# A selective-scan kernel: the order of the quarter loads of delta * u

## The chip, the cores and the metric

The kernel runs on one core of a Trainium2 chip. The time is device microseconds of one execution. Time before: 12,278.37 us, the median of three runs (12,270.65 to 12,295.46). One further execution was taken with the hardware profiler; all views below are of that one.

## The reference

Four layers work on images x of shape (4, 64, 64, 96). The first two (L0, L1) are state-space layers: normalise, project 96 channels to 2 x 192, convolve 3 x 3, and scan the 4096 pixels of each image in K = 4 directions (rows, columns, and both backwards), with 16 states per channel. Cut to the scan, which is where the change lies:

```python
def step(h, inp):
    u, d, b, c = inp
    dA = jnp.exp(d[..., None] * A)
    h = dA * h + d[..., None] * b[:, :, None, :] * u[..., None]
    y = jnp.einsum('bken,bkn->bke', h, c)
    return (h, y)
```

Here u is the convolved image in the order of the direction, d is delta (softplus of a small projection, one value per channel and pixel), b and c are 16 values per pixel, and A is a constant per channel and state. The product d * u doesn't depend on the state: it has one value per image, direction, channel and pixel, and every one of the 16 states needs the same value. Afterwards the four directions are added, normalised, gated and projected back. Layers L2 and L3 are attention without softmax and a quantised two-layer network on the same pixels; the change doesn't touch them.

## The kernel before

The two state-space layers are each done for two pairs of images, which gives four phases one after the other. A phase has three parts: `prepare` (normalisation, convolution, delta, b, c), `scan_phase`, and `finish`, which runs beside the next phase's `prepare`. The token layers L2 and L3 come at the end.

`prepare` leaves its results in DRAM. For every chunk of TC = 512 pixels there is one tensor `delta` (bf16, in three parts that add up to fp32) and one tensor `du` with delta * u in fp32. `du` holds two copies of the same data, copy 0 and copy 1; the first index of the tensor is the copy (lines 160 to 162, written at lines 321 and 322). Within a copy, the second index g runs over the G = 8 combinations of direction and image, then come the channels and the pixels.

`scan_phase` (line 471) cuts the work into units: 8 chunks x 16 blocks of EB = 12 channels, 128 units in a phase, 512 in all. The 128 partitions of a unit are 16 states x 8 combinations g. They fall into four quarters of 32 partitions; a quarter is 4 states x 8 combinations. So each of the 8 rows of `du` is wanted in 4 partitions of each quarter. `load` (line 386) takes the tile h of a unit, 128 x 12 x 512 fp32, issues the load of the delta tile (72 partitions, line 379), and then fills h with six loads on SP's DMA queue (line 401). `load_quarters` reads `du` with a broadcast over 4 states. The middle two quarters (partitions 32 to 95) are filled together, from copy 0 and copy 1; a single quarter is filled from one copy only, copy `first % 2`. Each is split in two halves of 6 channels by the loop over e. One middle load moves 768 KB, one quarter load 384 KB, in rows of 12,288 B.

The loop over a unit's 12 channels n then interleaves these steps on five engines, in an order that is written out by hand (`manual_schedule`):

- POOL multiplies three channels of h by b at a time (`times_b`, line 411), half a unit ahead of the scan. Its first two products of a unit read the first half of h, its last two the second.
- TensorE spreads delta over the states (`replicate`, line 417), ScalarE turns it into exp(delta * A) (`decay`, line 421).
- VectorE runs the recurrence over 512 pixels in place in h (`scan`, line 428), with the carry of the chunk before.
- TensorE contracts the finished unit with c (`contract`, line 446), ScalarE evicts (line 458), and at the end of the unit SP stores y in four pieces (`store`, line 466).

At the last channel of unit `at`, SP issues the store of unit at - 1 and then the loads of unit at + 3 (lines 532 to 539); h has four buffers. So SP's DMA queue holds in each unit one delta load, six h loads and four y stores, and now and then a load of b or c. A DMA takes one of eight semaphores in turn; SP waits before it issues a DMA until the DMA before it on the same semaphore has landed.

Of the kernel before, what the change touches and what calls it, by code (L numbers as in the profile page):

```python
# [82 lines left out]
class Consts:  # L83
# [3 lines left out]
    def load(self, pool, name, shape):  # L87
        t = pool.tile(shape, F32, name=name)
        self.nc.sync.dma_start(t, self.a[name])
        return t  # L90
# [40 lines left out]
class Scans:  # L131
# [19 lines left out]
    def prepare(self, ph):  # L151
# [16 lines left out]
        with self.tc.tile_pool(name="prep", bufs=1) as wp, self.tc.tile_pool(  # L168
# [3 lines left out]
            def load(name, shape, at=0):  # L172
                t = wp.tile([at + shape[0]] + shape[1:], F32, name=name)
                nc.sync.dma_start(t[at:], a[pre + name])
                return t

            xp = load("x_proj", [C, 2, 2, XD2])
            dt_w = load("dt_w", [XD2 - 2 * NS, 2, E], at=2 * NS)
            conv_b = load("conv_b", [C, 2])
            ds = load("Ds", [C, 2, K])  # L180
            dsum = wp.tile([C, 2], F32, name="dsum")
# [204 lines left out]
    def load(self, u):  # L386

        nc, ph = self.nc, u.ph
        u.h = self.units.tile([128, EB, TC], F32, name="h", bufs=4)
        self.load_delta(u)  # L390
        n = EB // 2
        for first, quarters in ((1, 2), (3, 1), (0, 1)):
            for e in range(0, EB, n):
                self.load_quarters(u, e, n, first, quarters)

# [595 lines left out]
```

## Time and profile before

| | |
|---|---|
| median of three runs | 12,278.37 us |
| profiled execution | 12,285.39 us, its span 12,283.6 us |
| scan phases, from first to last scan of each | 784 to 2659, 3596 to 5467, 6406 to 8279, 9215 to 11,088 us |
| VectorE busy in the steady stretch of the first phase (812 to 2540 us) | 1661.90 of 1728 us |
| POOL busy there | 1614.88 us |
| ScalarE busy there | 1182.33 us |
| TensorE matmul busy there, granted clock | 1332.07 us, 0.90 |
| share of the 16 DMA engines there, bytes | 0.74, 252 GB/s |

How to read the views. The profile names engines PE (matmul), PEld (weight load), DVE (VectorE), ACT (ScalarE), POOL (GpSimd) and SPq (SP's instruction queue). A row of the costliest groups gives line, engine, operation, output <- inputs with partitions x elements, the count, busy time in us, mean ns of one, and then the idle time just ahead of it with what ended it. The chain of waits goes back from the last instruction to whatever released it, step by step, and gives shares of the span; "DMA h<-du" there is time between the issue and the landing of an h load. A line of the waits reads: who waited, for whom, us in total, times, longest. A line of the timeline gives start, duration, engine, line, operation and count, and in brackets the idle time before it. A wait for several things is put down to the one that seems to have come last, so a name in brackets may be a neighbour of the true cause. The trace also holds one record for each DMA packet (start, duration, bytes) and one for each part of a load that lands.

### The profile page before, as it was taken

How to read it: one execution, taken by the hardware profiler on the slowest of the kernel's cores; microseconds unless marked ns; L12 is line 12 of the kernel's file. 1: busy time of each engine (PE TensorE's matmuls, PEld its weight loads, DVE VectorE, ACT ScalarE, POOL GpSimd, SP SyncE). 2: the span in 40 equal slices, each digit the busy share in tenths (PEclk: the TensorE clock that was granted, in tenths of full speed). 3: DMA queues.
4: the chain of work that ended last, by engine and by line, in shares of the span. 5: the costliest groups of instructions: out<-in, count | busy, mean ns of one | idle time of the engine just before them, and what ended most of it. 6: DMA issues, size and time to landing. Idle time of an engine off the chain costs nothing.

```text
span 12283.6 us, 340681 instructions
## 1 busy us (share of the span) xinstructions
PE 9393.5 (76%) x147008; PEld 4897.8 (40%) x147008; DVE 9369.7 (76%) x9235; ACT 7066.9 (58%) x11815; POOL 7389.7 (60%) x2316
## 2 busy tenths in 40 slices
PE   7757777769877777769877777778877777777777
PEld 2224444433334444433334444443334444444333
DVE  2479999963569999982569999993459999993667
ACT  2456666643456666653456666662446666662556
POOL 0159999950149999970129999980119999990000
PEclk8669898889778988889778988888778888988787
DMA  3577777754667777764667777764567777773110
GB/s 94 170 226 256 251 252 252 251 166 140 205 206 253 251 252 255 252 201 123 183 206 253 252 251 254 251 226 125 173 194 250 253 253 252 252 252 124 19 21 11
DMA packets 906195, 2491.48 MB, mean 203 GB/s; under 512 B 278030, under 2 KB 560756, under 8 KB 773236
## 3 DMA queue, kind: packets, MB, share of 16 engines
q1 hardware_dynamic: 578036, 2163.43, 52.6%
q10 hardware_dynamic: 326656, 306.25, 8.5%
q8 instruction: 1158, 18.97, 0.7%
q14 instruction: 345, 2.83, 0.1%
HBM read 1955.47 MB, written 513.80 MB: 201 GB/s over the span
## 4 chain that ended last, share of the span: by engine, by line
DMA 57%; PE 20%; SPq 9%; DVE 5%; ACT 4%; issue 3%; POOL 1%; ACTq 1%; DVEq 0%; POOLq 0%
DMA h<-du 51%; SPq L401 8%; PE c L263 8%; PE f L596 2%; PE d L309 2%; DMA yk<-y 2%; DMA delta<-parts 1%; PE c L292 1%; PE f L687 1%; PE f L605 1%; DMA du<-du_sb 1%; POOL parts L323 1%; PE f L676 1%; DVE parts L324 1%; PE f L662 1%
## 5 line engine op out<-in xcount | busy, mean ns | idle before, releaser
L411 POOL TENSOR_TENSOR h<-h,b 128x1536 f32<-128x1536 f32 x2048 | 7019.3, 3461 | 603.8 <-DMA h<-du 230.7
L428 DVE TENSOR_TENSOR_SCAN h<-a,carry,h 128x512 f32<-128x512 f32 x5376 | 6346.6, 1259 | 238.3 <-POOL h L411 231.9
L421 ACT ACTIVATE a<-a,a_col 128x512 f32<-128x512 f32 x6144 | 4030.4, 664 | 1917.7 <-PE a L417 1885.8
L446 PEld LDWEIGHTS y<-h,cw 128*32 128x32 f32 x131072 | 2789.8, 129 | 3520.4 <-issue 1302.1
L446 PE MATMUL y<-h,cw 128*32 128x48 f32 x131072 | 3663.3, 266 | 537.8 <-DVE h L428 210.6
L417 PE MATMUL a<-dlt,rep 72*128 72x512 bf16 x6144 | 2562.4, 428 | 1339.9 <-DVE h L428 1242.8
L323 POOL CAST parts<-dl 96x1024 bf16<-96x1024 f32 x256 | 342.1, 1351 | 3108.6 <-DVE dl L320 2742.6
L319 DVE TENSOR_TENSOR du_sb<-dl,xc 96x1024 f32<-96x1024 f32 x256 | 397.0, 1577 | 1294.6 <-ACT dl L317 1242.0
L458 ACT COPY d<-y 128x384 f32<-128x384 f32 x2048 | 979.7, 478 | 490.5 <-PE y L446 449.4
L263 PE MATMUL c<-xn,taps 96*96 96x512 f32 x2304 | 1036.8, 611 | 73.7 <-DVE xn L248 52.8
L428 DVE TENSOR_TENSOR_SCAN h<-a,h 128x512 f32<-128x512 f32 x768 | 873.0, 1203 | 176.9 <-ACT a L421 139.2
L417 PEld LDWEIGHTS <-rep 72*128 72x128 bf16 x6144 | 490.8, 99 | 888.7 <-issue 646.5
L309 PE MATMUL d<-xd,dt_w 7*96 7x512 f32 x1024 | 523.0, 859 | 260.0 <-ACT xd L295 227.4
L263 PEld LDWEIGHTS c<-xn,taps 96*96 96x96 f32 x2304 | 383.6, 168 | 709.9 <-issue 631.2
L828 POOL MEMSET tn<- 1x4096 f32 x8 | 28.0, 3533 | 863.2 <-PE pa L848 514.2
L270 ACT ACTIVATE xc<-c,conv_b 96x512 f32<-96x512 f32 x128 | 87.3, 682 | 716.0 <-PE c L263 646.4
L596 PE MATMUL f<-yk,perm 128*128 128x384 f32 x1024 | 417.3, 547 | 96.6 <-DMA yk<-y 87.2
L324 DVE TENSOR_TENSOR parts<-dl,parts 96x1024 bf16<-96x1024 f32 x256 | 366.9, 1455 | 154.3 <-POOL parts L323 154.3
L317 ACT ACTIVATE dl<-d 96x1024 f32<-96x1024 f32 x256 | 252.0, 1017 | 402.3 <-DMA delta<-parts 230.6
L292 PE MATMUL c<-xc,x_proj 96*103 96x512 f32 x512 | 422.1, 961 | 2.5 <-ACT xc L270 2.5
L309 PEld LDWEIGHTS d<-xd,dt_w 7*96 7x96 f32 x1024 | 152.3, 212 | 548.3 <-ACT xd L295 299.0
L363 ACT ACTIVATE cw<-c,gmask 128x256 f32<-128x256 f32 x512 | 285.7, 569 | 119.2 <-DMA c<-bc 61.9
(114 smaller groups left out, 5656.7 us busy)
## 6 DMA issues: line engine op xcount, KB each, us to landing
h<-du SPq DMA_DIRECT2D x1024, 768.0 KB
h<-du SPq DMA_DIRECT2D x2048, 384.0 KB
delta<-parts ACTq DMA_DIRECT2D x512, 288.0 KB
dlt<-delta SPq DMA_DIRECT2D x512, 288.0 KB
du<-du_sb SPq DMA_DIRECT2D x256, 384.0 KB
du<-du_sb ACTq DMA_DIRECT2D x256, 384.0 KB
y<-d SPq DMA_DIRECT2D x2048, 48.0 KB
yk<-y SPq DMA_DIRECT2D x256, 384.0 KB
```

The costliest lines, as they stand in the source:

```text
L263: nc.tensor.matmul(rows(ps[:C]), taps[:, tap, h * C : (h + 1) * C], xn[:, ROWS * c + dy : ROWS * (c + 1) + dy, dx : dx + HW], start=tap == ...
L292: nc.tensor.matmul(rows(ps[:XD2]), xp[:, k, h], u[:, h], start=h == 0, stop=h == 1)
L309: nc.tensor.matmul(ps[:, m], dt_w[part, k, m * C : (m + 1) * C], xd[part], start=True, stop=True)
L324: nc.vector.tensor_tensor(parts[:, 2], delta, parts[:, 1], ALU.subtract)
L401: self.nc.sync.dma_start(u.h[32 * first : 32 * (first + quarters), e : e + n].rearrange("p e t -> p (e t)"), source.rearrange("a g e t -> ...
L411: self.nc.gpsimd.tensor_tensor(h, h, b, ALU.mult)
L417: self.nc.tensor.matmul(u.a[n], self.cst.rep[:, h], u.dl[:, e], start=True, stop=True)
L421: self.nc.scalar.activation(u.a[n], u.a[n], AF.Exp, scale=u.ph.a_col[:, at : at + 1])
L428: self.nc.vector.tensor_tensor_scan(u.h[:, n], u.a.pop(n), u.h[:, n], 0.0 if u.c == 0 else u.ph.carry[:, at : at + 1], ALU.mult, ALU.add,)
L446: self.nc.tensor.matmul(view(u.y[32 * j : 32 * j + 32], l2 * EB, (8 * EB, 4), (1, EB)), u.ph.cw[u.c][:, l1, 8 * j + l2], view(u.h, 64 * l1 ...
L458: self.nc.scalar.copy(u.d[:, :, :, l1], u.y[:, : 32 * EB].rearrange("p (t h x) -> p t h x", t=4, h=2))
L596: nc.tensor.matmul(ps[:, : 4 * C].rearrange("p (w v e) -> p w v e", w=4, v=nv), cst.perm[:, k], view(t, off, (sw if k < 2 else -sw, 4), (1 ...
```

## The change

The loop in `load` that fills h names the quarters in another order. Before, after the middle two quarters came quarter 3 (partitions 96 to 127, from copy 1) and then quarter 0 (partitions 0 to 31, from copy 0); now quarter 0 comes ahead of quarter 3. Number, size and issue order of the loads by halves stay as they are.

```diff
@@ -389,7 +389,7 @@
         u.h = self.units.tile([128, EB, TC], F32, name="h", bufs=4)
         self.load_delta(u)
         n = EB // 2
-        for first, quarters in ((1, 2), (3, 1), (0, 1)):
+        for first, quarters in ((1, 2), (0, 1), (3, 1)):
             for e in range(0, EB, n):
                 self.load_quarters(u, e, n, first, quarters)
```

## The prediction

> **What bounds the kernel now.** I read the times first (median 12,278.37 us, three runs from 12,270.65 to 12,295.46; that spread of 0.2% is about what a measurement of this kernel can tell from no change), then the chain of waits and the costliest groups of the page:
>
> ```profile
> DMA 57%; PE 20%; SPq 9%; DVE 5%; ACT 4%; issue 3%; POOL 1%; ACTq 1%; DVEq 0%; POOLq 0%
> DMA h<-du 51%; SPq L401 8%; PE c L263 8%; PE f L596 2%; PE d L309 2%; DMA yk<-y 2%; DMA delta<-parts 1%; PE c L292 1%; PE f L687 1%; PE f L605 1%; DMA du<-du_sb 1%; POOL parts L323 1%; PE f L676 1%; DVE parts L324 1%; PE f L662 1%
> ...
> L411 POOL TENSOR_TENSOR h<-h,b 128x1536 f32<-128x1536 f32 x2048 | 7019.3, 3461 | 603.8 <-DMA h<-du 230.7
> L428 DVE TENSOR_TENSOR_SCAN h<-a,carry,h 128x512 f32<-128x512 f32 x5376 | 6346.6, 1259 | 238.3 <-POOL h L411 231.9
> ```
>
> Half of the chain is the very load that the change reorders; VectorE sat idle mostly for POOL, POOL mostly for that load. Next the queue's own waits of SP, and the timelines of POOL, VectorE and SP in one steady stretch:
>
> ```profile
> SPq L401 <- DMA h<-du: 2362.9, 1448, 3.9
> ```
>
> ```profile
> 1307.83 14.21 DVE L428 TENSOR_TENSOR_SCAN h<-a,carry,h 128x512 f32<-128x512 f32 x12 [0.39 <-POOL h L411]
> 1323.91 38.94 DVE L428 TENSOR_TENSOR_SCAN h<-a,carry,h 128x512 f32<-128x512 f32 x33 [1.87 <-POOL h L411]
> ```
>
> ```profile
> 1320.42 13.68 POOL L411 TENSOR_TENSOR h<-h,b 128x1536 f32<-128x1536 f32 x4 [2.35 <-ACT d L458]
> 1334.28 13.71 POOL L411 TENSOR_TENSOR h<-h,b 128x1536 f32<-128x1536 f32 x4 [0.18 <-DMA h<-du]
> ```
>
> ```profile
> 1331.25 8.01 SPq L401 DMA_DIRECT2D h<-du  x6
> 1339.36 3.24 SPq L466 DMA_DIRECT2D y<-d  x4
> 1343.94 0.81 SPq L379 DMA_DIRECT2D dlt<-delta  x1
> 1345.80 7.89 SPq L401 DMA_DIRECT2D h<-du  x6
> ```
>
> A unit (12 channels x 512 steps) costs VectorE 14.2 us when nothing stops it and POOL 13.7 us. The records of the trace, over 464 steady units (8 to 123 of each phase), give a period of 14.69 us, so about 0.49 us is lost. I call a unit's six h loads m0, m1 (middle 64 rows, first and second half), a0, a1 (next quarter) and b0, b1 (last quarter). In 84% of these units POOL's first product starts within 0.35 us of the landing of b0. The "ACT d" named above is not its cause: the 2.35 us ended when b0 landed. SP holds at most eight loads in flight: m0 of the next unit goes out when a1 has landed, m1 when b0 has landed. So the loads set the pace.
>
> They do so through single DMA engines. m0 and m1 land in 16 parts, each single quarter in only 8 (and one write made at once). The packets of 12,288 B take 460 ns at best (26.7 GB/s), also when 16 engines run; the four quarter loads land 1.87 to 1.90 us apart on the typical engine up to b0, which is 4 x 0.46: the same eight engines do them one after the other. The last engine to land is the one that counts. Its spacings are m0 to m1 1.97 us, to a0 1.88, to a1 1.90, to b0 2.63, to b1 2.47: slow only in the b pair, when the next unit's delta load and m0 have started on the other engines.
>
> [...] At that moment only about three engines carry 12,288 B packets, and these take 0.56 to 0.90 us, so total bandwidth is not the reason.
>
> **The change part by part.** Removed and added: nothing. Every engine issues the same instructions in the same order with the same waits; only the rows and the copy of du behind loads 3 to 6 are exchanged. 2048 loads are touched (512 units x 4), 384 KB each, same issue time. POOL's r0 needs m0, the a and the b of the first half whichever quarter comes last. So at equal transfer speed the step costs 0 us, hidden by nothing because nothing is moved.
>
> [...]
>
> 1. Delta against b, taken away. The b pair of the last engine has 2.63 + 2.47 - 2 x 4 x 0.46 = 1.42 us above the packet times. Part is instruction fetching: 2.11 packets of 16,384 B a unit, at 26.7 GB/s 0.61 us each, spread evenly 2.11 x 0.61 x 5.1 / 14.69 = 0.45 us in that stretch (estimate). 0.97 us is left. [...] -0.97 us a unit. Bounds 0 (the slowness lies on the memory side) to -0.97.
>
> 2. Middle loads against b, added. m0 of the next unit goes out 0.29 us after a1 landed and lands on the typical engine 5.6 us after its issue; the last engine's b0 lands 2.3 us and its b1 4.8 us after that same issue. So b1 lies wholly beside m0. [...] Bounds 0 [...] to +1.84. [...] +1.45 us.
>
> 3. Start of a0 beside the tail of m1's upper half[...]. The last engine reaches a0 late and shows 1.88 us, 0.04 above the packets: at most -0.04 us, taken as 0.
>
> Net 1.45 - 0.97 = +0.48 us a unit on the engine that is never idle: its own packets, 24 x 0.46 + delta 6 x 0.16 + output stores 16 x 0.036 + fetching 1.29, are 13.9 of the 14.69 us. What is late next: b1, hence a0 of the next unit, which SP sends when b1 has landed, then b0, then POOL's first product, then VectorE. Steady units 496 (124 x 4): 496 x 0.48 = 238 us. At each phase start two further units are loaded back to back without a delta gain of note: 4 x 2 x 1.45 = 12 us. Sum 250 us on the profiled execution's own 12,285.39 us (span 12,283.6), 12,535; that run lies 7 us above the median, so 12,528 us.
>
> **The rivals.** (a) [...] both orders meet the same congestion in memory: the same bytes at the same instants, 12,278 us. [...] Against: the b pair is slowed at low total traffic. Chance 0.14. (b) Faster: the delta conflict goes but m0's upper half yields[...]. It decides where the added overlap is below 0.97 us. The gain ends at VectorE's 14.2 us: 496 x -0.49 = -243, 12,035 us; halfway 12,157. Chance 0.22. (c) Much slower: the b pair's 0.97 us was memory, stays, and the whole 1.84 us comes on top: 496 x 1.84 = +913, 13,190 us. Chance 0.07. The forecast itself has 0.57, with its own range from +0.1 us (12,328) to +0.87 us (1.84 - 0.97; 12,278 + 432 = 12,710).
>
> **How the numbers follow.** Slower by over 0.2% holds the forecast and (c): 0.64. Within 0.2% (25 us) holds (a): 0.14. Faster holds (b): 0.22. The range of 8 in 10 runs from 12,130, which leaves out about half of (b), to 12,760, which leaves out (c).
>
> **What would show it.** In the profile after: the same counts in every row of the groups; POOL's mean near 3461 ns and the scan's near 1259 ns; more idle time ahead of L411 and L428; the time that SP waits for h loads at L401 up from 2362.9 us. In the landing records: a0 to a1 still about 1.9 us, a1 to b0 nearer 1.9 than 2.63 (step 1), b0 to b1 well above 2.47 (step 2), period near 15.2 us. Unchanged spacings would mean (a); a b pair under 5.1 us together with a period near 14.2 us would mean (b). [...]

## The result, and the profile after

The changed kernel takes 12,199.1 us (median of four runs, 12,184.87 to 12,209.92) against 12,276.8 us for the kernel before (12,270.65 to 12,295.46): ratio 0.9933, interval 0.9916 to 0.9951. It is faster by 0.67%; forecast was slower by 2.0%. The profiled execution took 12,191.39 us, 94 us less than that of before. From the first to the last scan of each phase, summed over the four phases, the trace gives 7490.6 us before and 7416.3 us after: 74 us of the 94 lie there. The other 20 us lie outside, where nothing was changed; another kernel with the same order (the second experiment) has 4799.6 us outside the scans, against 4793.0 before and 4773.3 after, so this part is what two executions differ by.

The chain of waits and the costliest groups of the changed kernel, the lines that answer to those of before:

```profile
DMA 57%; PE 20%; SPq 9%; DVE 5%; ACT 4%; issue 3%; POOL 1%; ACTq 1%; DVEq 0%; POOLq 0%
DMA h<-du 52%; SPq L401 9%; PE c L263 8%; PE f L596 2%; PE d L309 2%; DMA yk<-y 1%; PE c L292 1%; DMA delta<-parts 1%; PE f L605 1%; PE f L687 1%; PE f L676 1%; POOL parts L323 1%; DVE parts L324 1%; PE f L662 1%; PE ph L806 1%
...
L411 POOL TENSOR_TENSOR h<-h,b 128x1536 f32<-128x1536 f32 x2048 | 7021.7, 3462 | 527.6 <-DMA h<-du 187.1
L428 DVE TENSOR_TENSOR_SCAN h<-a,carry,h 128x512 f32<-128x512 f32 x5376 | 6347.5, 1259 | 176.7 <-POOL h L411 174.0
```

Counts and durations are those of before (3461 and 1259 ns a piece there); only the idle time ahead of the two groups fell, POOL's from 603.8 to 527.6 us and VectorE's from 238.3 to 176.7 us. The loads of h still set the pace: half of the chain is theirs. The page alone can't tell more. SP's own waits, from the queue's view, even point the other way:

```profile
SPq L401 <- DMA h<-du: 2480.7, 1444, 4.4
```

SP waits longer at the h loads than before (2362.9 us), in a faster kernel. So here the wait of the issuing queue does not tell which kernel is slower. The timelines of VectorE and then POOL, in the stretch that was shown of before, are only a sample:

```profile
1299.71 44.73 DVE L428 TENSOR_TENSOR_SCAN h<-a,carry,h 128x512 f32<-128x512 f32 x38
1344.68 36.53 DVE L428 TENSOR_TENSOR_SCAN h<-a,carry,h 128x512 f32<-128x512 f32 x31 [0.23 <-POOL h L411]
```

```profile
1298.13 41.17 POOL L411 TENSOR_TENSOR h<-h,b 128x1536 f32<-128x1536 f32 x12
1341.21 24.13 POOL L411 TENSOR_TENSOR h<-h,b 128x1536 f32<-128x1536 f32 x7 [1.90 <-DMA y<-d]
```

VectorE runs 38 scans without a gap of note, POOL twelve products; then POOL stops for 1.90 us. What ended that stop was b0 of a unit, which landed 0.31 us before the product started; the "y<-d" in brackets is a neighbour.

What tells the kernels apart is the landing records of the h loads. The table has, for 464 steady units, the mean time between the landings of the last DMA engine (m0, m1: middle rows; a0, a1: the single quarter that comes first; b0, b1: the one that comes last; 0 and 1 are the halves), how far the last engine is behind the typical one at b1, and VectorE's period from unit to unit, all in us. The cycle's other three stretches, m0 to m1, m1 to a0 and a0 to a1, are given in the text where they matter. Ratios are to the kernel before. The experiments are in it too.

| kernel | a1 to b0 | b0 to b1 | b1 to next m0 | behind at b1 | period | ratio |
|---|---|---|---|---|---|---|
| before | 2.63 | 2.47 | 3.84 | 3.29 | 14.70 | 1 |
| changed | 2.28 | 3.07 | 3.48 | 3.67 | 14.56 | 0.9933 |
| e1 order of before, copies exchanged | 2.60 | 2.49 | 3.83 | 3.33 | 14.70 | 1.0002 |
| e2 changed order, copies exchanged | 2.32 | 3.08 | 3.46 | 3.72 | 14.57 | 0.9927 |
| e3 order of before, small delta | 1.85 | 1.93 | 4.20 | 1.06 | 14.05 | 0.9732 |
| e4 changed order, small delta | 1.89 | 1.97 | 4.67 | 0.98 | 14.05 | 0.9731 |
| e5 order of before, no upper middle | 2.59 | 2.39 | 3.71 | 3.50 | 14.44 | 0.9896 |
| e6 changed order, no upper middle | 1.98 | 1.97 | 4.30 | 1.39 | 14.06 | 0.9737 |
| e7 order of before, delta between | 3.32* | 1.92 | 2.57* | 1.98 | 14.18 | 0.9784 |
| e8 changed order, delta between | 2.98* | 3.44 | 2.09* | 5.23 | 15.62 | 1.0335 |
| e9 order of before, delta on rows 56 to 127 | 1.93 | 2.42 | 3.89 | 2.32 | 14.14 | 0.9786 |
| e10 changed order, delta on rows 56 to 127 | 2.67 | 3.71 | 3.51 | 4.85 | 15.62 | 1.0359 |

(* The delta load, 6 x 0.16 us on each of its engines, lies in a1 to b0 here, in b1 to m0 elsewhere.)

So the change did shorten a1 to b0 by 0.35 us and lengthen b0 to b1 by 0.60 us, as the prediction said it would; but b1 to the next m0 fell by 0.36 us, m0 to m1 by 0.07, and the period by 0.13 us. Over 512 units that is 67 us of the 74 us that the scan phases got shorter.

### The profile page after: what moved, and what is told of

It reads as the page before. It is cut to its first block, busy times and chain, and to the rows that moved or that the text cites. A ratio compares the mean times of both kernels' runs of the same rounds, so it can differ in the third digit from the quotient of the medians.

```text
span 12189.6 us, 340681 instructions
## 1 busy us (share of the span) xinstructions
PE 9338.7 (77%) x147008; PEld 4884.4 (40%) x147008; DVE 9363.7 (77%) x9235; ACT 7063.0 (58%) x11815; POOL 7391.0 (61%) x2316
## 4 chain that ended last, share of the span: by engine, by line
DMA 57%; PE 20%; SPq 9%; DVE 5%; ACT 4%; issue 3%; POOL 1%; ACTq 1%; DVEq 0%; POOLq 0%
DMA h<-du 52%; SPq L401 9%; PE c L263 8%; PE f L596 2%; PE d L309 2%; DMA yk<-y 1%; PE c L292 1%; DMA delta<-parts 1%; PE f L605 1%; PE f L687 1%; PE f L676 1%; POOL parts L323 1%; DVE parts L324 1%; PE f L662 1%; PE ph L806 1%
## 5 line engine op out<-in xcount | busy, mean ns | idle before, releaser
L411 POOL TENSOR_TENSOR h<-h,b 128x1536 f32<-128x1536 f32 x2048 | 7021.7, 3462 | 527.6 <-DMA h<-du 187.1
L428 DVE TENSOR_TENSOR_SCAN h<-a,carry,h 128x512 f32<-128x512 f32 x5376 | 6347.5, 1259 | 176.7 <-POOL h L411 174.0
L417 PE MATMUL a<-dlt,rep 72*128 72x512 bf16 x6144 | 2529.7, 422 | 1315.1 <-DVE h L428 1228.6
```

The lines of the kernel that those rows point to most:

```text
L411: self.nc.gpsimd.tensor_tensor(h, h, b, ALU.mult)
L417: self.nc.tensor.matmul(u.a[n], self.cst.rep[:, h], u.dl[:, e], start=True, stop=True)
L428: self.nc.vector.tensor_tensor_scan(u.h[:, n], u.a.pop(n), u.h[:, n], 0.0 if u.c == 0 else u.ph.carry[:, at : at + 1], ALU.mult, ALU.add,)
```

## Experiments: is it the rows or the copy?

The change exchanges two things at once: the rows of SBUF that are written and the copy of `du` that is read. The first pair keeps the orders and exchanges the copies alone.

```diff
-        copies = slice(0, 2) if quarters == 2 else slice(first % 2, first % 2 + 1)
+        copies = slice(0, 2) if quarters == 2 else slice(1 - first % 2, 2 - first % 2)
```

> The order of before (quarter 3, then quarter 0), but quarter 3 is read from copy 0 of du and quarter 0 from copy 1. Theory P (what counts is the rows written[...]): nothing changes against before, ratio 1.000 within 0.002, spacings of the last engine a1 to b0 about 2.6 us and b0 to b1 about 2.5 us, period 14.69 us. Theory M (what counts is which copy in DRAM is read late, beside the next unit's middle load): it behaves as the changed kernel, ratio about 0.993, a1 to b0 about 2.3 us, b0 to b1 about 3.1 us.

> The changed order (quarter 0, then quarter 3), with the copies exchanged as in the run before it. Theory P: as the changed kernel, ratio 0.993, a1 to b0 2.3 us, b0 to b1 3.1 us, period 14.56 us. Theory M: as the kernel before, ratio 1.000, a1 to b0 2.6 us. If both matter, each of these two runs lies between.

Measured: e1 is 1.0002 (0.9994 to 1.0010), e2 is 0.9927 (0.9911 to 0.9944). Their spacings agree with those of before and of the changed kernel within 0.04 us. The groups of e1, then of e2:

```profile
L411 POOL TENSOR_TENSOR h<-h,b 128x1536 f32<-128x1536 f32 x2048 | 7020.8, 3462 | 601.5 <-DMA h<-du 227.7
L428 DVE TENSOR_TENSOR_SCAN h<-a,carry,h 128x512 f32<-128x512 f32 x5376 | 6348.1, 1259 | 237.8 <-POOL h L411 234.9
```

```profile
L411 POOL TENSOR_TENSOR h<-h,b 128x1536 f32<-128x1536 f32 x2048 | 7022.0, 3462 | 530.0 <-DMA h<-du 204.9
L428 DVE TENSOR_TENSOR_SCAN h<-a,carry,h 128x512 f32<-128x512 f32 x5376 | 6350.9, 1260 | 174.8 <-POOL h L411 171.7
```

The idle time follows the rows (601.5 and 530.0 us; before 603.8, after 527.6), not the copy. Which copy in DRAM is read makes no difference that these runs can tell.

## Experiments: take each supposed partner of the conflict away

The second pair takes away most of the delta load:

```diff
...
+        if u.c == 0 and u.eb == 0:
+            self.dl0 = self.units.tile([DROWS, DC, TC], BF16, name="dlt", bufs=1)
+            nc.sync.dma_start(self.dl0.rearrange("p e t -> p (e t)"), of)
+        else:
+            few = self.units.tile([DROWS, 128], BF16, name="few", bufs=3)
+            nc.sync.dma_start(few, of[:, :, :128])
+        u.dl = self.dl0
```

> The order of before, but the delta tile is loaded in full only for the first unit of a phase and used for all; every other unit's delta load brings 256 B a row in place of 4096 B (wrong decay in all units but the first, same instructions elsewhere, same number of loads). Theory P: the b pair of the last engine loses its conflict with the delta rows: a1 to b0 falls from 2.63 to about 2.0 us and b0 to b1 from 2.47 to about 2.1 us, the engine also has 0.9 us less of its own, so the period goes to VectorE's own 14.2 us: 512 x 0.45 = 230 us less, about 12,045 us. Theory M: delta takes no part in it; the engine only saves its own 0.9 us, the spacings of the b pair stay near 2.6 and 2.5 us.

> The changed order with the same small delta loads (wrong decay in all units but the first of a phase). Theory P: the changed order had its gain from escaping delta, so nothing of the gain is left: a1 to b0 about 2.0 us as in the run before it, b0 to b1 stays near 3.0 us for the conflict with the upper half of the next middle load, so the b pair is about 0.9 us longer than in the run before it and the time the same or up to 200 us more. Theory M: the b pair keeps the difference that the two full kernels have (0.25 us longer in the changed order), and this run is as fast as the run before it or faster.

Measured: 0.9732 (0.9720 to 0.9745) and 0.9731 (0.9719 to 0.9744), the same. The scan's group in e3, then in e4:

```profile
L431 DVE TENSOR_TENSOR_SCAN h<-a,carry,h 128x512 f32<-128x512 f32 x5376 | 6317.3, 1256 | 0.0
```

```profile
L431 DVE TENSOR_TENSOR_SCAN h<-a,carry,h 128x512 f32<-128x512 f32 x5376 | 6317.3, 1260 | 0.0
```

VectorE has no idle time left ahead of these scans; the period of 14.05 us is its own, 0.15 us less than the 14.2 us that I had read from the timeline. In e3 the b pair fell to nearly the bare packet times (1.85 and 1.93 us against 1.84). That alone does not show delta as the cause: with VectorE setting the pace the loads have slack, and the next unit's m0 is issued 2.39 us after a1 has landed instead of 0.29, so that load is taken away from b as well. The runs that move delta, below, test it by itself. In e4 the expectation that b0 to b1 would stay near 3.0 us is refuted: it is 1.97 us. The last engine is only 1.0 us behind the others instead of 3.7, m0 is issued 2.94 us after a1 instead of 0.35, and its first part lands 3.46 us after b1. So b is over before the next unit's middle load is under way, and the conflict of step 2 does not take place.

The third pair leaves out the upper half of the middle load from the fifth unit of a phase on (the four buffers of h are fixed tiles, whose rows 64 to 95 keep what was there):

```diff
+            if quarters == 2 and i >= 4:
+                quarters = 1
```

> The order of before; from the fifth unit of each phase on, the middle load fills rows 32 to 63 alone[...] (rows 64 to 95 keep what an earlier unit left, so a quarter of the states is wrong; the tile h is four fixed buffers for that). [...] Theory P: [...] nothing changes for the late engine: a1 to b0 about 2.6 us, b0 to b1 about 2.4 us, period 14.6 to 14.7 us, ratio 0.995 to 1.00. A theory in which the late engine suffers from the sheer number of packets in memory: a b pair near 4.2 us and a ratio under 0.98.

> The changed order with the same cut of the middle load. Theory P with the conflict of step 2 [...]: that conflict is gone, b0 to b1 falls from 3.07 to about 2.1 us, the late engine is no longer the limit and the period goes to the 14.03 us seen with small delta loads: ratio about 0.975. If step 2 of the prediction doesn't exist, b0 to b1 stays at 3.0 us and the ratio at 0.993.

Measured: e5 is 0.9896 (0.9880 to 0.9913), e6 is 0.9737 (0.9723 to 0.9752). The scan's group of e5, then that of e6 with its chain of waits:

```profile
L433 DVE TENSOR_TENSOR_SCAN h<-a,carry,h 128x512 f32<-128x512 f32 x5376 | 6335.6, 1258 | 134.6 <-POOL h L416 132.8
```

```profile
DVE h L433 17%; DMA h<-du 14%; PE c L263 8%; PE y L451 8%; DMA y<-d 6%; ACT a L426 3%; PE a L422 3%; ACT d L463 3%; PE f L601 3%; SPq L406 2%; PE d L309 2%; SPq L471 2%; DMA yk<-y 1%; PE c L292 1%; DMA delta<-parts 1%
...
L433 DVE TENSOR_TENSOR_SCAN h<-a,carry,h 128x512 f32<-128x512 f32 x5376 | 6317.4, 1254 | 0.0
```

In e6 the h loads are no longer the chain (14% in place of 52%) and VectorE no longer waits. The same bytes left out of both orders: the order of before gains 1.0%, the changed one 2.0% of its time (0.9737 / 0.9933 = 0.980). The b pair of e5 hardly moved (4.98 against 5.10 us). Its period fell by 0.26 us, more than the 0.1 us at most that was expected; the other half of that lies in other stretches, with a quarter of the h bytes gone. The b pair of e6 fell from 5.35 to 3.95 us. So the upper half of the middle load costs the changed order's b pair 1.40 us and that of before 0.12 us. In e6, too, the loads have slack and m0 goes out later, 2.08 us after a1, so part of the 1.40 us may be that.

## Experiments: move delta, in the queue and in SBUF

If b in partitions 0 to 31 suffers from delta and b in partitions 96 to 127 from the next middle load, the old order with delta out of b's way should beat both kernels. First the place in the queue:

```diff
-        self.load_delta(u)
         n = EB // 2
         for first, quarters in ((1, 2), (3, 1), (0, 1)):
+            if first == 0:
+                self.load_delta(u)
```

(in the changed order `if first == 3`).

> The order of before with the delta load issued between the two single quarters: middle, quarter 3, delta, quarter 0. Same loads, same bytes, full result. Theory P: the late engine is some 2.5 us behind the others, so when these write delta [...] it is still on quarter 3 [...], and b comes after it: most of the delta conflict is gone without the conflict of the changed order. Period 14.1 to 14.4 us, ratio 0.975 to 0.985. If the delta load costs the same wherever it stands in the queue: ratio 1.00.

> The changed order with the delta load between the single quarters: middle, quarter 0, delta, quarter 3. Theory P: the late engine is on quarter 0 [...] when the others write delta, so the delta conflict comes back, and the conflict of quarter 3 with the next middle load stays: slower than the changed kernel, ratio to before 0.998 to 1.02. If only the distance of the delta load from the end of the unit counts: as the run before it.

Measured: e7 is 0.9784 (0.9770 to 0.9799), 12,015 us; e8 is 1.0335 (1.0313 to 1.0356), 12,689 us. The scan's group of e7, then POOL's and the scan's of e8:

```profile
L429 DVE TENSOR_TENSOR_SCAN h<-a,carry,h 128x512 f32<-128x512 f32 x5376 | 6322.4, 1256 | 23.9 <-POOL h L412 22.8
```

```profile
L412 POOL TENSOR_TENSOR h<-h,b 128x1536 f32<-128x1536 f32 x2048 | 7013.8, 3458 | 1046.5 <-DMA h<-du 363.7
L429 DVE TENSOR_TENSOR_SCAN h<-a,carry,h 128x512 f32<-128x512 f32 x5376 | 6364.7, 1259 | 637.7 <-POOL h L412 627.1
```

The same move of the same load takes 2.2% off one order and adds 4.0% to the other (1.0335 / 0.9933). VectorE's idle time goes to 23.9 us in the one and to 637.7 us in the other. The sign was foreseen, the size in e8 was not: 1.0335 lies above the 1.02 that I had set as the upper end. POOL's timeline in e8 shows what a unit looks like there:

```profile
1312.41 13.70 POOL L412 TENSOR_TENSOR h<-h,b 128x1536 f32<-128x1536 f32 x4 [1.52 <-DMA h<-du]
1327.48 13.71 POOL L412 TENSOR_TENSOR h<-h,b 128x1536 f32<-128x1536 f32 x4 [1.36 <-DMA h<-du]
1344.23 13.69 POOL L412 TENSOR_TENSOR h<-h,b 128x1536 f32<-128x1536 f32 x4 [3.04 <-PE a L418]
```

POOL's four products take the same 13.7 us as ever; ahead of the three shown it stands still 1.4 to 3.0 us. In 97% of the steady units of e8 its first product starts within 0.35 us of the landing of b0. The delta conflict came back in another place than b: m1 to a0 is 3.06 us here against 1.89 in the changed kernel. There the late engine is at quarter 0, as the expectation said.

Then the place in SBUF, with delta where it was in the queue (the tiles are fixed, their rows 0 to 55 are zero, and so are these rows of the spreading matrix):

```diff
-            u.dl.rearrange("p e t -> p (e t)"),
+            u.dl[128 - DROWS :].rearrange("p e t -> p (e t)"),
```

> The order of before, delta in its old place in the queue, but its 72 rows stand on partitions 56 to 127 in place of 0 to 71 ([...] TensorE multiplies with 128 rows, the others zero). Full result. Theory P: b [...] meets neither delta nor the upper half of the middle load, so the b pair of the last engine falls from 5.10 to 4.0 to 4.2 us and the period to 14.05 to 14.2 us: ratio 0.973 to 0.98. If [...] the moment at which delta is read from memory: nothing changes, ratio 1.00.

> The changed order with delta on partitions 56 to 127. Theory P: b (quarter 3[...]) now meets both delta (1.0 us) and the upper half of the next middle load (1.4 us): b pair about 6.3 us, period 15.2 to 15.7 us, ratio to before 1.02 to 1.045, slower by 3 to 5% than the changed kernel. If the moment of the memory read counts: as the changed kernel, 0.993.

Measured: e9 is 0.9786 (0.9773 to 0.9800), 12,006 us; e10 is 1.0359 (1.0345 to 1.0373), 12,708 us. The scan's group of e9, then of e10:

```profile
L430 DVE TENSOR_TENSOR_SCAN h<-a,carry,h 128x512 f32<-128x512 f32 x5376 | 6319.3, 1273 | 12.7 <-POOL h L413 12.7
```

```profile
L430 DVE TENSOR_TENSOR_SCAN h<-a,carry,h 128x512 f32<-128x512 f32 x5376 | 6364.9, 1261 | 632.4 <-POOL h L413 620.3
```

Nothing was moved here in the queue or in DRAM; 72 rows of a tile stand elsewhere. TensorE also multiplies with 128 rows in place of 72, but in both kernels alike, and they go opposite ways. In the old order the b pair falls from 5.10 to 4.35 us, less than the 4.0 to 4.2 us expected: a1 to b0 goes from 2.63 to 1.93 us, near the packet times, but b0 to b1 only from 2.47 to 2.42. What still slows b1 there is not shown. In the changed order b meets delta and the middle load (6.38 us, expected about 6.3). e7 and e9 give the full result and beat both kernels, by 1.5% against the changed one (0.9784 / 0.9933 = 0.985).

## Why the prediction was wrong, point by point

**What bounds the kernel: right.** The h loads set the pace, and POOL's first product waits for b0: within 0.35 us of its landing in 84% of the steady units before and 93% after. Where an experiment freed the loads, VectorE's idle time went to nothing.

**What the change exchanges: right.** Same instructions, other rows. e1 and e2 (1.0002 and 0.9927) rule out the copy in DRAM. e9 and e10 show that the rows of delta matter with its place in the queue unchanged: rows 0 to 71 and rows 56 to 127 make a difference of 2.1% in one order and 4.3% (1.0359 / 0.9933) in the other, with opposite signs. What it is in these rows that makes one load slow another no record shows.

**Step 1, delta against b, -0.97 us: right in place, and about right in size.** That all of the 0.97 us left over is delta's, and goes with it, was the author's estimate. Moved to partitions 56 to 127, delta costs the pair 6.38 - 5.35 = 1.03 us in e10, where b is in 96 to 127; in e9, where b is in 0 to 31, it saves 5.10 - 4.35 = 0.75 us. With the upper middle left out of both, the b pair is 4.98 us in partitions 0 to 31 and 3.95 us in 96 to 127, 1.03 us apart. The way to 0.97 was partly luck. It took a packet of instruction fetching to last 0.61 us; the records of before show 1.13 us on average. And it put 0.45 us of the pair down to fetching, but the 105 steady units in which no such packet falls in that stretch still have a pair of 4.96 us, against 5.10 for all.

**Step 2, the middle load against b, +1.45 us: right in place, at the upper end in size.** The upper bound of 1.84 us, four packets of 0.46 us, and the 1.45 us taken of it were the author's estimate; the trace of before has no b pair in partitions 96 to 127. Between the changed kernel and e6 it is 5.35 - 3.95 = 1.40 us, with the later m0 in it. Against e9, where b also keeps clear of delta and m0 goes out 0.35 us after a1 as in the changed kernel, it is 5.35 - 4.35 = 1.00 us. With e9 as the measure, the two steps are -0.75 and +1.00 us and add up to the 0.25 us by which the pair did grow. In e4, where the loads have slack, step 2 costs nothing.

**The step that failed is the sum, "Net 1.45 - 0.97 = +0.48 us a unit on the engine that is never idle".** It treats the b pair's delay as if it were added to the period. Measured, the pair became longer by 0.25 us (5.10 to 5.35) and the period shorter by 0.13 us, since b1 to the next m0 lost 0.36 us. That is so in every pair with delta at full size and both halves of the middle load: the order with quarter 3 last has this stretch shorter by 0.36 (changed against before), 0.37 (e2 against e1), 0.38 (e10 against e9) and 0.48 us (e8 against e7). The prediction has no term for this stretch and so put it at no change, without a reason. It is the term that turned the sign; the pair's own +0.25 us in place of +0.48 would still have meant slower.

Why that stretch shrinks is open. One reading, which no record shows, is that an engine whose writes are held up gets on with what stands next in its queue, and so gives part of the delay back. In e8 the stretch is 2.09 us, less than the packets that every one of the eight engines has in it if they follow one another, 16 x 0.036 + 4 x 0.46 = 2.42 us (an estimate from the packet times), so part of that work seems to be under way before b1 has landed. But that is no mark of a held-up b: in e7, where b0 to b1 is 1.92 us and hardly slowed, 56% of the units are below 2.42 us too. Within the changed kernel units with a longer b pair do have a shorter stretch after it (correlation -0.43; before -0.14), which fits the reading and proves nothing. The other reading is that the engine that is last at b1 is not the one that is last at m0: at b1 the last engine is further behind the typical one in the changed kernel (3.67 us against 3.29), at the next m0 it is not (3.03 us against 3.18). The records don't name engines. Delta's own speed isn't the reason: its packets took 229 ns on average before and 202 after, but 230 ns in e10, where the stretch is short all the same.

A second assumption in the sum is weak too. I spoke of one late engine that is never idle and also bears the instruction fetching. With 1.13 us for each of its 2.11 fetch packets its work would be 24 x 0.46 + 6 x 0.16 + 16 x 0.036 + 2.38 = 14.96 us a unit, more than the 14.70 us that a unit takes (an estimate from the packet times), so it can't bear them all one after the other. Sorted by how many fetch packets start between two landings of b0, the units of before take 14.03 us with one, 14.50 with two and 15.65 with three (47, 320 and 97 units); those of the changed kernel 13.96, 14.52 and 14.96 (20, 374 and 70 units). So with one or two packets the orders cost the same, and the whole gain lies in the units with three; e1 (14.13, 14.57, 15.48) and e2 (14.12, 14.56, 14.76) repeat it. This is a sorting and no experiment, since a longer unit also has more room for a third packet. It says that the sum left out how fetching and the order of the quarters act together. Before and after, one to three engines are over 1 us late at b1 in most units; which of them bears the fetching stays open.

**Step 3 and the start of a phase:** too small to be told apart here. Step 3's stretch, m1 to a0, is 1.88 us before and 1.89 after.

**The rivals.** (a), that both orders meet the same congestion, is refuted: e9 and e10 differ from their originals by the rows of delta and by a wider matmul that both have, and go opposite ways. (c), that delta's part is memory and stays, is refuted by e9, where 0.75 us of it goes with the rows; for what is left in b0 to b1 memory isn't ruled out. The low traffic that the prediction speaks of is that of a moment: before, 3.9 packets of 12,288 B were under way on average 1.5 us after the landing of a1, and 13.7 of them 4 us after it, with b1 among them. (b) came closest, with the right sign, but its mechanism is not what the runs show: it wanted the added overlap below 0.97 us; the runs give 1.00 to 1.40 us, and it was the stretch after b that shrank. The floor it went to was wrong as well, 14.05 us and not 14.2.

## What to carry to other kernels

When loads set the pace, as they do here, look at the last engine to land, not at the mean of all: in the steady stretch from 812 to 2540 us the DMA engines were busy 0.74 of the time before, 0.74 in the changed kernel and 0.75 in e9. In this kernel it paid to keep the rows of a small load away from those of the quarter that lands last: moving delta to partitions 56 to 127 took 2.1% off the order whose last quarter is in 0 to 31 and added 4.3% to the one whose last quarter is in 96 to 127. And a delay on one stretch of a queue isn't yet a delay of the loop: sum over the whole cycle before giving it a sign.

## What the runs showed of the hardware that was not expected

- A load of 288 KB per unit, about 8% of the bytes on the queue, cost the kernel before 2% by the rows it was written to: 12,271 us with delta on partitions 0 to 71, 12,006 us on 56 to 127 (e9 and its runs of before).
- A conflict of the same loads cost b 1.00 to 1.40 us a unit or nothing, by what stood around it: in the changed kernel the last engine was 3.7 us behind and m0 went out 0.35 us after a1; in e4 it was 1.0 us behind and m0 went out 2.94 us after a1. The runs don't separate the lateness from the later m0.
- Packets of 12,288 B took 464 ns (median, 26.5 GB/s) in the kernel before and 462 ns in e6, where each steady h load lands in 8 parts and none in 16. So an engine's packets took the same time with 8 engines at work on h as with 16.
